# A four-layer network on one core: the spreading product and the state sums get due times of their own, single steps are queued by known work, and two tiles are doubled

## The chip, the cores and the metric

The kernel runs on one core of a Trainium2 chip. A core has TensorE (PE, matrix products into the PSUM memory), VectorE (DVE), ScalarE (ACT), GpSimd (POOL) and SyncE (SP, which here only issues DMAs). Each engine works through its own queue in the order in which the program was written out, and waits at the head of the queue until what the next instruction needs is there. The metric is the device time of one execution in microseconds, the median of the runs shown; less is better.

## What is computed

The input is `x` of shape 4 x 96 x 64 x 64 (4 images, 96 channels, 4096 pixels). Four layers are added to it, one after the other:

```python
x = x + _L0_conv_ref(_gn(x), ...)      # layer norm, 1x1 projection, 3x3 depthwise convolution, selective scan
x = x + _L1_conv_ref(_gn(x), ...)      # deformable 3x3 convolution, 4 bilinear corners for 9 taps
t = t + _L2_attn_ref(_ln_t(t), ...)    # FFT over the 4096 tokens, a product by channel, inverse FFT
t = t + _L2_ffn_ref(_ln_t(t), ...)     # 96 -> 384 -> 96 with quantized numbers
t = t + _L3_attn_ref(_ln_t(t), ...)    # attention without softmax, 6 heads
t = t + _L3_ffn_ref(_ln_t(t), ...)     # as the other one
```

The core of layer 0 is a recurrence along 4096 pixels, for 4 images, 4 directions, 192 channels and 16 states:

```python
dA = jnp.exp(d_t[..., None] * A)
h = dA * h + (d_t * u_t)[..., None] * b_t[:, :, None, :]
y = jnp.einsum('bkdn,bkn->bkd', h, c_t)
```

## The kernel before, in words

**Units of the scan.** The recurrence is cut into 1536 units (4 images x 4 directions x 4 stretches of 1024 pixels x 24 groups of 8 channels; 8 channels x 16 states fill the 128 partitions). `Layer0.scan` (L887) writes them out one after the other. A unit has these parts, each a method with a line of its own in the profile:

- `fetch` (L953) loads `da`, the step widths, 512 KB, from ACT's DMA queue (L982); `decay` (L1000) turns it into `exp(A * d)` on ACT (L1003).
- `inflow` (L1005) is the spreading product: two matmuls (L1009) that spread `du` of 8 channels over 128 partitions into the PSUM tile `db`. There are two `db` tiles, so the product of unit n+2 has to wait until the scan of unit n has read its tile.
- `enter` (L1018) multiplies `db` by `b_t` on DVE (L1023), and `recur` (L1025) runs the recurrence itself on DVE (L1031) into `hh`. There are six `hh` tiles.
- `weigh` (L1035) multiplies `hh` by `c_t` on POOL (L1040), and keeps the last state (L1038).
- `total` (L1042) is the state sums: for two units at a time, four matmuls (L1059) that add up the 16 states into the PSUM tile `py`; the first total of a block of eight units also adds an earlier result (L1054). An `hh` tile is free after its total. `settle` (L1067) copies `py` out on ACT (L1070), and `store` writes it.

**Side work.** Everything else is called side work here: the convolution (L752) and the gates of layer 0 for later images (`steps`, L812 to L884), the end of layer 0 (`behind`, L1081), layer 1 (`Layer1`; its samples are gathered at L1372 and transposed at L1405), and layers 2 and 3 (`Fourier`, `Ffn`, `LinearAttention`). It comes in two streams (L1792 on): `ends` holds the beginning of layer 0 and then layers 2 and 3 image by image; `middle` holds `behind` and layer 1 image by image. Layers 2 and 3 of an image begin when `middle` has sampled it.

**The order.** The whole order of instructions is decided while the program is built, by a planner in Python. Its `Clock` (L206) adds a fixed cost in us for every step to the end of the engine (`ends`), and gives every unit at least `PACE` = 4.5. After a unit of the scan, `yield True` (L949) hands over to the two streams, and as many side steps are written out as `has_room` (L231) lets in: an engine that the step uses may be planned at most `AHEAD` = 3, 3, 5 and 7 us (PE, DVE, ACT, POOL) past now, and DVE gets at most `BESIDE` = 6 us of side work for each unit. Inside a `pipe` (L272), which interleaves several chains of steps, `has_room` asks with the work that the same step had the last time. A single step outside a pipe is asked for in `Stream.step` (L331) with 1 us on all four engines, whatever it uses. Banks of PSUM for side work are counted too: three during the scan.

In iteration n, `scan` wrote out first `inflow` of unit n+1 and `decay` of unit n+2, on odd n `total` of units n-5 and n-4, then the loads, `recur` of unit n, `weigh` of unit n-2 and, where due, `settle` and `store`; then the side work of this iteration. `enter` of unit n+1 is written out either in the middle of the side work, ahead of a step that uses DVE, when the planner's clock has reached `entered` (the end of that unit's spreading product by the clock), or after the side work. The spreading product of unit n+1 therefore stood behind all side matmuls that were written out in iteration n-1.

**After the last unit** the banks of the scan go to the stream `ends` (`own_banks`, L1837), and what is left of the side work is written out alone: the end of layer 0 and layer 1 of the last image in one stream, layers 2 and 3 of the last images in the other.

**The doubled tiles.** In `steps`, the logarithm's tiles `lw` and `w1` (L833 to L842) exist once, and a token `lw=1` lets one chain at a time from the matmul at L829 to L842. In `Fourier.half`, the last stage (`last`, L1573) copies a product (L1579) to the single tile `yt` (L1581), which the next product reads (L1584); a token `yt=1` keeps a second chain from beginning its product before.

Of the kernel before, what the change touches and what calls it, by code (L numbers as in the profile page):

```python
# [1 line left out]

# [1 line left out]

# [4 lines left out]
F32 = mybir.dt.float32  # L9
# [10 lines left out]
B, C, H, W = 4, 96, 64, 64  # L20
# [174 lines left out]
PE, DVE, ACT, POOL = range(4)  # L195
# [10 lines left out]
class Clock:  # L206
# [4 lines left out]
    def __init__(self):  # L211
# [8 lines left out]

        self.enter, self.entered = None, 0.0

    def now(self):
        return max(self.ends[DVE], self.due) if self.own is None else self.own

# [15 lines left out]
    def precede(self, work):  # L241


        if self.enter and work[DVE] and self.own is None and self.entered + MARGIN <= self.ends[DVE]:
            self.enter()

    def add(self, engine, us, ready):
        self.ends[engine] = max(self.ends[engine], ready) + us
# [72 lines left out]
    yield wait(max(0.0, end - clock.now()))  # L321


class Stream:


# [4 lines left out]
    def step(self):  # L331

        net = self.net
        net.stream = self
        if self.over or self.ready > net.clock.now():
            return False
        if not self.piped and not (net.has_bank() and net.clock.has_room((1.0,) * 4, self.ready)):
            return False
        step = next(self.work, False)
        if step is False:  # L340
            self.over = True
            return False
        self.piped = step is None or step is BLOCKED
        if isinstance(step, Step):
            self.ready = net.clock.queue(step, net.clock.now())
        return step is not BLOCKED

# [195 lines left out]
class Layer0:  # L543
# [54 lines left out]
    def first(self):  # L598


        net = self.net
        tc, nc = net.tc, net.nc
        b = 0
        with tc.tile_pool(name=f"l0u{b}", bufs=1) as up, tc.tile_pool(name=f"l0b{b}", bufs=1) as sm:
            us = []
            x = self.tokens(b, up, us)
            xp_a, xp_c = (net.load(q, sm) for q in ("xp_a", "xp_c"))
            dtw = net.load("dtw", sm)
            xdbl = {}
            with tc.tile_pool(name=f"l0a{b}", bufs=1) as big, tc.tile_pool(name=f"l0i{b}", bufs=1) as cp:  # L610
                pad = big.tile([C, PW, PW], F32, name=f"pad{b}", tag="pad")
                weights = self.conv_weights(b, cp)
                yield from self.normed_rows(b, x, pad)

                def rows_first():
                    yield self.conv(b, 0, pad, us, weights, cp)
                    for j in range(NCH):
                        if j + 1 < NCH:
                            yield self.conv(b, j + 1, pad, us, weights, cp)
                        yield self.projected(b, j, us, xp_a, xp_c, sm, xdbl, (0,), f"c{j}")  # L620
                        for ks in ((0,), (0, 2), (2,)):
                            yield self.steps(b, ks, j, us, dtw, sm, xdbl)

                tokens = {f"c{j}": 0 for j in range(NCH)}
                yield from pipe(
                    net, rows_first(), 6, every=2, lane=Layer0.conv.__code__,
                    ex=3, lw=1, rl=2, du=2, zt=1, **tokens,
                )

            def columns():  # L630
                for j in range(NCH):
                    yield self.projected(b, j, us, xp_a, xp_c, sm, xdbl, (1,))
                    for ks in ((1,), (1, 3), (3,)):
                        yield self.steps(b, ks, j, us, dtw, sm, xdbl)

            yield from pipe(net, columns(), 5, every=2, ex=3, lw=1, rl=2, du=2)

    def before(self, b):
        net = self.net
        tc, nc, ins = net.tc, net.nc, net.ins  # L640
        with tc.tile_pool(name=f"l0u{b}", bufs=1) as up:

            us = []
            yield from self.inputs(b, up, us)
            with tc.tile_pool(name=f"l0b{b}", bufs=1) as sm:
                xp_a, xp_c = (net.load(q, sm) for q in ("xp_a", "xp_c"))
                dtw = net.load("dtw", sm)
                yield wait(4.0)
                xdbl = {}

                def chains():
                    yield self.projected(b, 0, us, xp_a, xp_c, sm, xdbl, (1, 0))
                    for j in range(NCH):
                        for ks in ((1,), (0, 1), (3,), (2, 3), (0,), (2,)):
                            yield self.steps(b, ks, j, us, dtw, sm, xdbl)
                        if j + 1 < NCH:
                            yield self.projected(b, j + 1, us, xp_a, xp_c, sm, xdbl, (1, 0))

                yield from pipe(self.net, chains(), 5, every=2, ex=3, lw=1, rl=2, du=2)

    @staticmethod
    def rows(pad, j):
# [149 lines left out]
    def steps(self, b, ks, j, us, dtw, sm, xdbl):  # L812

        net = self.net
# [5 lines left out]
        def tile_of(name, bufs):  # L820
            return sm.tile([128, CH], F32, name=f"{name}{tk}", tag=name, bufs=bufs)
# [5 lines left out]
        for i, k in enumerate(ks):  # L827
            o, m = (pd[64 * i : 64 * i + 64], slice(128, DI)) if both else (pd, slice(0, 128))
            nc.tensor.matmul(o, lhsT=dtw[:, k, m], rhs=xdbl[k % 2, j], start=True, stop=True)  # L829
        ex = tile_of("ex", 3)  # L830
        nc.scalar.activation(ex, pd, AF.Abs)
        nc.scalar.activation(ex, ex, AF.Exp, scale=-1.0)
        lw, w1 = tile_of("lw", 1), tile_of("w1", 1)  # L833
        nc.scalar.activation(lw, ex, AF.Ln, bias=net.one)
        nc.scalar.activation(w1, ex, AF.Identity, bias=net.one)
        yield cost(pe=2.2 if both else 1.1, act=2.7, holds=1, takes="rl")
        rl = tile_of("rl", 2)
# [49 lines left out]
    def scan(self):  # L887


        units = [  # L890
            Unit(b, k, step, g, i, q)
            for b in range(B)
            for k in ((1, 3, 0, 2) if b else (0, 1, 3, 2))
            for step in range(NT)
            for g in range(NG)
            for i in range(4)
            for q in range(2)
        ]
        ahead = 5
        loaded = 0  # L900
        clock = self.net.clock

        def at(m):
            return units[m] if 0 <= m < len(units) else None

        def made(u):
            return all(
                (u.b, u.k, both, 2 * u.j + h) in self.ready for both in (False, True) for h in range(2)
            )

        for n in range(len(units) + 7):
            for m in range(loaded, min(n + ahead + 1, len(units))):
                while not made(units[m]):
                    yield False
            if n == 0:
                while loaded < ahead:
                    self.fetch(units[loaded], units[loaded - 1] if loaded else None)
                    loaded += 1
                self.decay(at(0))
                self.decay(at(1))  # L920
                self.inflow(at(0))
                self.next = at(0)
                self.enter()

            for period, tick, load in ((24, 12, self.fetch_step), (8, 2, self.fetch_block)):
                u = at(n - n % period + period)
                if n % period == tick and u is not None and made(u):
                    load(u)
            for stage, m in ((self.inflow, n + 1), (self.decay, n + 2)):
                if at(m) is not None:  # L930
                    stage(at(m))
            if n % 2 == 1 and at(n - 5) is not None:
                self.total(at(n - 5), at(n - 4))
            if loaded < len(units):
                self.fetch(units[loaded], units[loaded - 1])
                loaded += 1
            if at(n) is not None:
                self.recur(at(n), at(n - 6).summed if n >= 6 else 0.0)
            if at(n - 2) is not None:
                self.weigh(at(n - 2))  # L940
            if n % 2 == 0 and at(n - 6) is not None and at(n - 6).i == 3:
                self.settle(at(n - 6))
            if n % 2 == 1 and at(n - 7) is not None and at(n - 7).i == 3:
                self.store(at(n - 7))
            clock.unit(self.scanned[1])
            self.next = at(n + 1)
            if self.next is not None:
                clock.enter, clock.entered = self.enter, self.next.spread
            yield True  # L949
            if clock.enter:  # L950
                self.enter()
# [483 lines left out]
class Fourier:  # L1435
# [6 lines left out]
    def __init__(self, ctx, net):  # L1442
# [14 lines left out]

        self.w2 = wp.tile([C + 1, 2, 128], F32, name="w2e")
        nc.sync.dma_start(self.w2[:C], ins["w2"])
        self.yt = wp.tile([C + 1, 8, 64], F32, name="yt")  # L1460

    def prepare(self, tp):
        net = self.net
# [63 lines left out]
    def half(self, key, g, tv, t, pool, big):  # L1527
# [45 lines left out]
        def last(m):  # L1573
# [3 lines left out]
            pt = net.mm(f"yp{key}_{m}", C).rearrange("p (q k) -> p q k", k=64)  # L1577
            for q in range(8):
                nc.tensor.matmul(pt[:, q, :], lhsT=d[:, m + q, :], rhs=m2[:, q, :], start=True, stop=True)  # L1579
            yt = self.yt  # L1580
            nc.scalar.copy(yt[:C], pt)  # L1581
            yield cost(pe=1.7, act=0.6, new=True)
            po = net.mm(f"o{key}_{m}").rearrange("p (q k) -> p q k", k=64)
# [2 lines left out]
            nc.vector.tensor_add(to[:, m : m + 8, :], to[:, m : m + 8, :], po[:C])  # L1586
            yield cost(dve=1.25)

        yield from pipe(self.net, (last(m) for m in range(0, 64, 8)), 4, yt=1)


def normed(net, t, tl, key, pool):
# [272 lines left out]
```

## Time and profile before

| | before |
|---|---|
| median of 3 runs | 8710.01 us (8709.18 to 8720.84) |
| the profiled execution's own time | 8725.68 us |
| its span, first to last instruction | 8723.9 us |
| mean granted TensorE clock | 0.779 |
| busy: PE, DVE, ACT, POOL | 6608.9, 6836.1, 4925.0, 5608.7 us |
| first spreading product, last scan | 187.3 us, 7507.4 us |
| DVE multiplication by `b_t` (L1023), recurrence (L1031) | 1214 ns and 2285 to 2344 ns each |

The profile is read in this way. A line of a group names the line of the code, the engine, the operation and the tiles (written `out<-in`), the number of instructions, their busy time and the mean of one in ns; behind the bar stands the time that the engine sat idle just before them, and what ended it. A line of waits says which engine and tile waited for which other one: us in total, number of times, the longest. A line of the timeline has the start in us, the duration in us, the instruction, and in brackets the idle time before it. In the table by stage each engine has its busy time and, in brackets, its number of instructions; then come the granted TensorE clock (1 is full speed), the busy share of the 16 DMA engines, and GB/s.

### The profile page before, as it was taken

Reading aid. Unit: us, or ns where it says so; the run is one execution under the profiler, and the core shown is the slowest. Engines: PE = TensorE matmul, PEld = TensorE weight load, DVE = VectorE, ACT = ScalarE, POOL = GpSimd, SP = SyncE. Lnnn points to the kernel's source line nnn. Section 1 sums busy time; section 2 is a strip of 40 time slices with the busy share of each in tenths; the row PEclk is TensorE's granted clock in tenths of the full one; section 3 lists DMA queues with packets and bytes.
Section 4 is the critical chain, followed back from the end, with each engine's and each line's share of the span. In section 5 each row is a group of like instructions: output and inputs, shape, how many; then the busy total and the mean of one; then the engine's idle time right before and its main releaser. Section 6 shows DMA issues by size and latency. Waiting matters only on the chain.

```text
span 8723.9 us, 97214 instructions
## 1 busy us (share of the span) xinstructions
PE 6608.9 (76%) x31960; PEld 2859.5 (33%) x31960; DVE 6836.1 (78%) x5155; ACT 4925.0 (56%) x9030; POOL 5608.7 (64%) x4291
## 2 busy tenths in 40 slices
PE   6675777759767777887676788777778887789697
PEld 2211221112222332321222245422335541267383
DVE  2799889978799898778799888788988888547514
ACT  5554566636467776555577666454766665322323
POOL 0465566656579898656588887565888877347200
PEclk9765787769667777886687788776778887788788
DMA  3677678877789999766799988866879997355110
GB/s 94 160 206 186 167 199 218 211 169 193 181 217 242 242 239 231 177 169 178 194 244 239 236 222 215 188 173 165 215 207 233 229 224 170 90 153 172 56 54 13
DMA packets 773820, 1608.33 MB, mean 184 GB/s; under 512 B 264065, under 2 KB 355741, under 8 KB 771206
## 3 DMA queue, kind: packets, MB, share of 16 engines
q10 hardware_dynamic: 244224, 843.17, 38.3%
q1 hardware_dynamic: 455366, 532.37, 23.7%
q0 software_dynamic: 73728, 226.57, 9.8%
q8 instruction: 257, 4.21, 0.2%
q14 instruction: 245, 2.01, 0.1%
HBM read 1345.43 MB, written 256.29 MB: 184 GB/s over the span
## 4 chain that ended last, share of the span: by engine, by line
PE 25%; DVE 15%; DMA 7%; ACT 5%; issue 4%; SPq 1%; POOL 1%; ACTq 1%; DVEq 0%; POOLq 0%
DVE hh L1031 7%; DVE db L1023 4%; PE f L1499 3%; PE ps L1405 3%; PE py L1059 3%; PE pd L1421 2%; DMA da<-de 2%; ACT g L1384 1%; PE db L1009 1%; PE pc L752 1%; PE h L1540 1%; PE yp L1579 1%; DMA m<-in_dft 1%; ACT da L1003 1%; PE lnc L474 1%
## 5 line engine op out<-in xcount | busy, mean ns | idle before, releaser
L1040 POOL TENSOR_TENSOR hh<-hh,bc 128x1024 f32<-128x1024 f32 x1536 | 3661.0, 2386 | 377.2 <-DVE hh L1031 274.3
L1031 DVE TENSOR_TENSOR_SCAN hh<-da,st,db 128x1024 f32<-128x1024 f32 x1152 | 2700.6, 2344 | 189.4 <-PE py L1059 74.0
L1023 DVE TENSOR_TENSOR db<-db,bc 128x1024 f32<-128x1024 f32 x1536 | 1864.0, 1214 | 604.4 <-PE db L1009 602.7
L1003 ACT ACTIVATE da<-da,w_al 128x1024 f32<-128x1024 f32 x1536 | 1737.5, 1145 | 511.8 <-DMA da<-de 168.1
L1372 POOL DMA_INDIRECT g<-table,idx x1152 | 1212.7, 1053 | 373.8 <-issue 173.6
L1009 PE MATMUL db<-du,rep 24*128 24x512 bf16 x3072 | 710.0, 461 | 858.3 <-DVE hh L1031 803.5
L1059 PE MATMUL py<-hh,w_fold 128*32 128x512 f32 x6144 | 1107.7, 796 | 16.2 <-issue 11.5
L1384 ACT ACTIVATE g<-g,wt 128x96 f32<-128x96 f32 x3456 | 963.6, 364 | 136.9 <-PE py L1059 34.3
L1031 DVE TENSOR_TENSOR_SCAN hh<-da,db 128x1024 f32<-128x1024 f32 x384 | 877.3, 2285 | 84.6 <-PE py L1059 40.7
L1405 PE MATMUL ps<-w_ident,g 128*96 128x128 f32 x3744 | 736.1, 342 | 176.3 <-ACT g L1384 101.2
L1009 PEld LDWEIGHTS <-rep 24*128 24x128 bf16 x3072 | 159.6, 94 | 1963.0 <-issue 1289.7
L1038 POOL COPY st<-hh 128x1 f32<-128x1 f32 x1152 | 235.0, 204 | 741.5 <-DVE hh L1031 688.6
L1405 PEld LDWEIGHTS ps<-w_ident,g 128*96 128x96 f32 x3744 | 511.3, 149 | 548.6 <-ACT g L1384 239.0
L840 POOL TENSOR_TENSOR lw<-lw,w 128x512 f32<-128x512 f32 x192 | 243.9, 1270 | 683.7 <-DVE w L838 649.0
L752 PE MATMUL pc<-pad,wc 96*128 96x512 f32 x1152 | 579.6, 643 | 32.7 <-DMA wc<-wc_d 23.3
L871 PE MATMUL pr<-ex,w_ident 128*128 128x512 f32 x384 | 305.7, 889 | 174.7 <-DVE ex L861 81.9
L1413 ACT COPY st<-ps 96x384 f32<-96x384 f32 x384 | 178.8, 472 | 422.0 <-PE ps L1405 385.5
L752 PEld LDWEIGHTS pc<-pad,wc 96*128 96x128 f32 x1152 | 221.0, 202 | 361.5 <-issue 314.3
L829 PE MATMUL pd<-xd,w_dtw 103*64 103x512 f32 (+1 forms) x512 | 275.7, 821 | 52.7 <-DVE rl L842 18.8
L1421 PE MATMUL pd<-st,wdc 96*128 96x256 f32 x1152 | 308.9, 419 | 1.3 <-DVE d L1548 1.1
L1508 ACT COPY d<-f 128x512 f32<-128x512 f32 x192 | 111.9, 583 | 301.8 <-PE f L1499 297.1
L1059 PEld LDWEIGHTS py<-hh,w_fold 128*32 128x32 f32 x6144 | 158.5, 125 | 355.2 <-issue 282.9
(252 smaller groups left out, 8915.4 us busy)
## 6 DMA issues: line engine op xcount, KB each, us to landing
da<-de ACTq DMA_DIRECT2D x1536, 512.0 KB
du<-du SPq DMA_DIRECT2D x1536, 96.0 KB
bc<-bcd SPq DMA_DIRECT2D x128, 512.0 KB
y<-yb SPq DMA_DIRECT2D x384, 128.0 KB
de<-rl SPq DMA_DIRECT2D x128, 256.0 KB
m<-in_dft SPq DMA_DIRECT2D x128, 256.0 KB
ad<-y ACTq DMA_DIRECT2D x192, 128.0 KB
table<-pix SPq DMA_DIRECT2D x256, 96.0 KB
```

What stands on the lines that cost most here:

```text
L752: nc.tensor.matmul(pp, lhsT=wc[:, q, g * 128 : (g + 1) * 128], rhs=pad[:, r0 + dy : r0 + dy + NR, dx : dx + W], start=(q == 0), stop=(q == 8),
L871: nc.tensor.matmul(pr, lhsT=net.ident, rhs=ex, start=True, stop=False)
L1003: self.net.nc.scalar.activation(u.da, u.da, AF.Exp, scale=self.al[:, a : a + 1])
L1009: self.net.nc.tensor.matmul(db[:, h, :], lhsT=self.rep[64 * u.q + 32 * h : 64 * u.q + 32 * h + 24], rhs=u.du[64 * u.q + 32 * h : 64 * u.q ...
L1023: self.net.nc.vector.tensor_mul(u.db, u.db, u.bc[:, 0, :])
L1031: nc.vector.tensor_tensor_scan(u.along(u.hh), u.along(u.da), u.along(u.db), first, ALU.mult, ALU.add)
L1040: self.net.nc.gpsimd.tensor_mul(u.hh, u.hh, u.bc[:, 1, :])
L1059: nc.tensor.matmul(py[p0 : p0 + 32], lhsT=self.fold[:, u.i, :], rhs=hc[:, h * CH : (h + 1) * CH], start=u.sums["add"] is None and u.i == 0 ...
L1372: nc.gpsimd.indirect_dma_start(out=g[:, k, :], out_offset=None, in_=self.tables[b % 2], in_offset=bass.IndirectOffsetOnAxis(ap=idx[:, n : ...
L1384: nc.scalar.activation(pixel, pixel, AF.Identity, scale=wt[:, n, c : c + 1])
L1405: nc.tensor.matmul(pt[:, k, :], lhsT=g[:, k, c * C : (c + 1) * C], rhs=net.ident, is_transpose=True, start=(c == 0), stop=(c == corners - 1),)
L1421: nc.tensor.matmul(po, lhsT=wdc[:, k, :], rhs=st[:, k, :], start=(k == 0), stop=(k == 8))
```

## The change

It has four parts.

1. **Due times.** The clock gets a list `early`. At the end of iteration n, `scan` appends the spreading product of unit n+2, due when the planner's clock of PE reaches the end of the scan of unit n (`scanned[1]`), and on even n the total of units n-4 and n-3, due when both are weighed (and, for the first of a block, `py` is settled). `precede`, which is called ahead of each side step of a pipe, writes out what is due before a step that uses PE. What has not come up by the beginning of iteration n+1 is written out there, in the old place.
2. **Single steps.** `Stream.step` looks up, by the place in the code at which the stream stands (`place`), which work the step from there had the last time, and asks `has_room` with that. The first time it asks with 1 us on all engines as before. A step that is only a wait then needs no room.
3. **`lw` and `w1` get two buffers each**, and the token is 2.
4. **`yt` gets two halves**, taken in turn, and the token is 2.

No instruction is added or removed, and every side step does what it did.

```diff
+        self.early = []
...
         if self.enter and work[DVE] and self.own is None and self.entered + MARGIN <= self.ends[DVE]:
             self.enter()
+        if work[PE] and self.own is None:
+            for due in [e for e in self.early if e[0] <= self.ends[PE]]:
+                self.early.remove(due)
+                due[1]()
...
+def place(steps):
+
+    while steps.gi_yieldfrom is not None and hasattr(steps.gi_yieldfrom, "gi_code"):
+        steps = steps.gi_yieldfrom
+    return steps.gi_code, steps.gi_frame.f_lineno
...
-        if not self.piped and not (net.has_bank() and net.clock.has_room((1.0,) * 4, self.ready)):
+        here = place(self.work) if self.work.gi_frame else None
+        work = net.known.get(here, (1.0,) * 4)
+        if not self.piped and not (net.has_bank() and net.clock.has_room(work, self.ready)):
             return False
...
         if isinstance(step, Step):
+            if not self.piped:
+                net.known[here] = step.work
             self.ready = net.clock.queue(step, net.clock.now())
...
-                    ex=3, lw=1, rl=2, du=2, zt=1, **tokens,
+                    ex=3, lw=2, rl=2, du=2, zt=1, **tokens,
...
-        lw, w1 = tile_of("lw", 1), tile_of("w1", 1)
+        lw, w1 = tile_of("lw", 2), tile_of("w1", 2)
...
-            for stage, m in ((self.inflow, n + 1), (self.decay, n + 2)):
-                if at(m) is not None:
-                    stage(at(m))
-            if n % 2 == 1 and at(n - 5) is not None:
-                self.total(at(n - 5), at(n - 4))
+            while clock.early:
+                clock.early.pop(0)[1]()
+            if n == 0:
+                self.inflow(at(1))
+            if at(n + 2) is not None:
+                self.decay(at(n + 2))
...
+            if at(n + 2) is not None:
+                clock.early.append((self.scanned[1], partial(self.inflow, at(n + 2))))
+            if n % 2 == 0 and at(n - 4) is not None:
+                u, v = at(n - 4), at(n - 3)
+                clock.early.append((max(u.weighed, v.weighed, self.settled if u.i == 0 else 0.0), partial(self.total, u, v)))
             yield True
...
-        self.yt = wp.tile([C + 1, 8, 64], F32, name="yt")
+        self.yt = wp.tile([C + 1, 2, 8, 64], F32, name="yt")
...
-            yt = self.yt
+            yt = self.yt[:, m // 8 % 2]
...
-        yield from pipe(self.net, (last(m) for m in range(0, 64, 8)), 4, yt=1)
+        yield from pipe(self.net, (last(m) for m in range(0, 64, 8)), 4, yt=2)
```

More of the change, by code (lines that the diff above doesn't have):

```diff
@@ L1 @@
 from contextlib import ExitStack
+from functools import partial
 import numpy as np
@@ L634, in columns @@
                         yield self.steps(b, ks, j, us, dtw, sm, xdbl)
-            yield from pipe(net, columns(), 5, every=2, ex=3, lw=1, rl=2, du=2)
+            yield from pipe(net, columns(), 5, every=2, ex=3, lw=2, rl=2, du=2)
     def before(self, b):
@@ L657, in chains @@
                             yield self.projected(b, j + 1, us, xp_a, xp_c, sm, xdbl, (1, 0))
-                yield from pipe(self.net, chains(), 5, every=2, ex=3, lw=1, rl=2, du=2)
+                yield from pipe(self.net, chains(), 5, every=2, ex=3, lw=2, rl=2, du=2)
     @staticmethod
```

## The prediction, as it was put on record

> **What bounds the kernel now.** First I read the table by stage, cut at the first spreading product, the last scan and the end of sampling.
>
> ```profile
> 187.00:7507.00 7320.00, 5513.34 (x24611) 2146.92 (x24612) 6241.70 (x4238) 4456.49 (x8155) 5230.06 (x3963) 0.76 0.80 203
> 7507.00:8180.00 673.00, 547.95 (x3912) 379.89 (x3904) 393.19 (x564) 208.04 (x421) 361.96 (x312) 0.85 0.46 130
> 8180.00:8724.00 544.00, 423.24 (x3173) 283.44 (x3172) 168.66 (x293) 166.20 (x331) 7.66 (x2) 0.86 0.11 33
> ```
>
> The columns are PE, weight loads, DVE, ACT and POOL. The scan takes 7320 us, and in it DVE is busy for 6241.7, more than any other engine, and idle for 1078. So time can be won there only by closing DVE's gaps. After it DVE is busy for 58% and then 31%: there the chain goes through other engines. The waits say who opens the gaps (us, times, longest):
>
> ```profile
> PE db L1009 <- DVE hh L1031: 803.5, 429, 20.5
> ...
> DVE db L1023 <- PE db L1009: 602.7, 262, 26.0
> ...
> DVE hh L1031 <- PE py L1059: 114.8, 95, 8.1
> ```
>
> 602.7 of the 1078 us are DVE waiting for a spreading product, 114.8 for state sums (a free `hh` tile). The first line is the reverse: PE at the head of its queue waiting until a scan has freed a `db` tile. The timelines of PE and of DVE show one gap:
>
> ```profile
> 3721.13 0.60 PE L1009 MATMUL db<-du,rep 24*128 24x512 bf16 x2
> 3721.66 7.06 PE L752 MATMUL pc<-pad,wc 96*128 96x512 f32 x8
> 3728.66 0.39 PE L1009 MATMUL db<-du,rep 24*128 24x512 bf16 x2
> 3728.97 1.07 PE L1059 MATMUL py<-hh,w_fold 128*32 128x512 f32 x8
> ```
>
> ```profile
> 3723.15 2.35 DVE L1031 TENSOR_TENSOR_SCAN hh<-da,st,db 128x1024 f32<-128x1024 f32 x1
> 3729.09 1.23 DVE L1023 TENSOR_TENSOR db<-db,bc 128x1024 f32<-128x1024 f32 x1 [3.60 <-PE db L1009]
> ```
>
> Two `db` matmuls of 0.39 us stand behind 7.06 us of convolution; their tile had been free since before 3721.8, yet DVE, done at 3725.5, waits 3.60 us.
>
> Last, the final image's inverse Fourier stage:
>
> ```profile
> 8518.59 0.58 ACT L1581 COPY yt<-yp 96x512 f32<-96x512 f32 x1 [2.60 <-PE yp L1579]
> ...
> 8519.23 1.13 PE L1584 MATMUL o<-yt,w2e 97*128 97x512 f32 x2 [0.72 <-ACT yt L1581]
> ...
> 8520.19 1.50 PE L1579 MATMUL yp<-i,d 128*96 128x64 f32 x16
> ```
>
> PE idles 0.72 us in each round for the copy.
>
> **The change part by part.** The sum is made against the profiled execution's 8725.68 us (span 8723.9 plus 1.8), which is 15.7 above the median 8710.01.
>
> *Spreading products earlier.* From the built instruction order of both kernels I took, for each unit m, the side matmuls written out between scan m-2, which frees the tile, and the product of m, each at its line's mean PE time in the trace. Before: mean 3.24 us, 6.61 at the 90th percentile. After: 2.40 and 4.65. The product gains 0.84 us of lead, about 2 where the queue is longest. I set that against DVE's waits for it, counted singly in the trace from 0.15 us: 105 under 1 us (51 us in all), 56 of 1 to 2 (80), 81 of 2 to 5 (249), 19 longer (197). A lead of 0.84 takes about 45 from the first class and 56 x 0.84 = 47 from the second; about 1.4 each takes 113 from the third; 2 each takes 38 from the last, which is mostly PE standing still behind a side step whose load or POOL work is late. That is 243. Not all reaches the end: a scan that starts earlier meets its `da`, its `hh` or the next product sooner. Between all of it and a quarter (60) I take six tenths, since DVE's gaps have no second cause of this size: -146.
>
> What is queued behind it: the product waits for its scan at the head of PE's queue, and side matmuls stand behind. PE is free for 7320 - 5513 = 1807 us of the scan, of which 803 are such waits already; I count the rest as cover. Without it, see the rival below.
>
> [...] The rows show mean waits of 1.87 us (803.5/429), and 1004 us of PE's time that no `db` wait fills[...].
>
> *State sums earlier.* In the built order 44 of the 765 totals now come two units ahead of the old place, and 70 fewer come in the last possible one. Between 0 and -115 I take -35, a third, since most stay.
>
> *Two tiles for the gates, known work for single steps.* ACT waits for `lw` 66.5 us (49 times), DVE for `w` 38.8 in the scan. But ACT is busy for only 61% of it, and more chains compete for the same order. From +40 to -66 I take -5, near the DVE row. Single steps issue loads and norms sooner; the built order has image 1's Fourier transform begin at unit 1241 instead of 1315. That pays only at the end.
>
> *What is moved from the end into the scan.* Before, image 1's attention and second feed-forward are still open at the last scan; after, they are done, and so are 10 of 16 hidden groups of image 2's first half. In the scan they cost DVE 16 x 0.67 (L1603) + 8 x 1.54 (L1684) + 8 x 0.73 (L1740) + 10 x 0.54 (L1548) + 6 for two inverse roots = 41, and PE about 100, which PE's free time hides. DVE is the bound: +41. Their POOL and ACT steps lie in those engines' slack, and their loads (image 2's tokens, 1.5 MB, moved past SP's queue) come where DMA is 0.65 to 0.8 busy; both 0, up to +10.
>
> *The end.* Before, image 2's Fourier stage starts 192 us after the last scan (7699), and image 2 ends at 747 (8254), 100 us after the last sampled pixel at 647 (8154); only then is image 3 loaded. After, its Fourier stage runs from the start, so it ends at about 747 - 192 = 555 and sampling becomes the last: image 3 starts at 647, -100. Fourier matmuls now run beside the offset convolutions of image 3 (L1267), which may delay sampling by 0 to 40; I take 15: -85. With two `yt` halves the built order has pairs of products, so the 0.72 us are covered in 16 rounds of the last image: -11, I take -10.
>
> Sum: -146 - 35 - 5 + 41 - 85 - 10 = -240. 8725.7 - 240 = 8486 for a profiled execution; the median goes from 8710 to **8470**.
>
> **The rivals.**
>
> *The wait moves.* DVE gets its product sooner and waits as long for something else: side steps that stand behind PE's new waits, or `da`, whose DMAs share engines 0.80 busy, over 0.90 in the sampling stretches. Speaks for it: in the table by stage, from 2500 to 3250, DVE is already busy for 92% and POOL for 89%. Against it: in the trace six tenths of the waits for products lie outside the sampling stretches (2500 to 3500, 4250 to 5500, 6000 to 7250). Then only the end gains: -95 + 41 = -54, 8656.
>
> *The lead is enough.* Once PE is ahead it stays ahead. All waits under 5 us for products go (380) and half of those for sums (57): -437 + 41 - 110 = -506, 8204. For it: PE has 1807 us free. Against it: side bursts like the 7.06 us above remain.
>
> *Slower: PE's queue is blocked.* In the sum over 1534 units the products move ahead of 4974 - 3675 = 1300 us of side matmuls. If PE reaches each of them early and stands there, its waits grow by 1300: 5513 + 803 + 1300 = 7616 against 7320, +296 on the scan. With the end's -95 that is 8911. It decides from 1004 us of new waits on, 77% of the 1300; below that PE's free time takes it. Against it: a product is written out only once the clock puts PE past the scan.
>
> *It does nothing:* the due times are mostly not reached and the order stays. The built order excludes most of that: 61% of the products now stand ahead of the scan before them, against 43%. 8710.
>
> **How the numbers follow.** Chances: the forecast 0.62, the wait moves 0.17, the lead is enough 0.12, nothing 0.03, blocked 0.06. The forecast's own bounds: -243 to -60 for products, -115 to 0 for sums, -66 to +40 for tiles, [...]-125 to -50 for the end; taken together, since they don't all fall on one side, 8350 to 8590. To leave out no more than 2 in 10, the range runs from 8290, part of the way to the second rival, to 8660, which takes in the first. A measurement of this kernel tells about 0.2% (17 us) from no change: faster 0.91, same 0.03, slower 0.06.
>
> **What would show it.** Right: DVE's wait for `db` at about 350 to 450 us instead of 603; PE's wait for the scan at 900 to 1500, up from 803; the last scan at about 7360; image 3's load about 650 us after it instead of 750; rounds of the `yt` stage without PE's 0.72. Wrong: `db` waits gone but the scan as long (the wait moved), side work's waits on DVE far above the scan's 214 us, a granted clock well below 0.76, or sampling ending later than 690 us after the last scan.

## The result, and the profile after

The changed kernel takes 8602.1 us (median of 4 runs, 8574.27 to 8630.86). The ratio to the kernel before is 0.9871, 95% interval 0.9837 to 0.9905: 113 us faster than the kernel before, whose median with a fourth run is 8715.0, where 240 were forecast. The profiled execution took 8605.6 us (span 8603.8), 120.1 less than the one before. Line numbers have moved: the spreading product is L1033, its multiplication L1047, the scan L1055, the sums L1083 (L1078 at the start of a block).

The table by stage of the changed kernel, cut at its first and last scan and at the load of image 3 (PE, weight loads, DVE, ACT, POOL, clock, DMA share, GB/s):

```profile
180.00:7516.00 7336.00, 5572.59 (x25022) 2188.87 (x25023) 6290.54 (x4290) 4505.53 (x8269) 5252.58 (x3980) 0.77 0.80 203
7516.00:8170.00 654.00, 529.93 (x3650) 373.61 (x3647) 376.68 (x540) 197.75 (x401) 364.48 (x311) 0.82 0.47 131
8170.00:8604.00 434.00, 359.52 (x3028) 253.35 (x3028) 126.35 (x217) 137.29 (x270) 3.83 (x1) 0.90 0.13 37
```

The scan is not shorter: 7336 us against 7319. The last scan ends at 7516.2, before at 7509.7. The gain lies behind it: 1087.6 us against 1214.1, which is 126.5 less. Ahead of it another 10 us are gone (the first scan starts at 180.3 instead of 190.3), and the scan itself gives 16.5 back. DVE's waits inside the scan:

```profile
DVE hh L1055 <- PE py L1083: 323.0, 132, 14.8
DVE db L1047 <- PE db L1033: 247.9, 95, 22.9
DVE hh L1055 <- ACT da L1027: 82.7, 62, 11.0
```

Waits for products have fallen from 602.7 to 247.9. Waits for sums have risen from 114.8 to 323.0 and those for `da` from 13.3 to 82.7. PE's wait for the scan is 763.5, before 803.5. One gap in the timelines of PE and of DVE, in the same kind of stretch as the one shown before:

```profile
3689.62 0.39 PE L1033 MATMUL db<-du,rep 24*128 24x512 bf16 x2
3690.46 4.56 PE L770 MATMUL pc<-pad,wc 96*128 96x512 f32 x10 [0.46 <-ACT xa L780]
3694.95 1.07 PE L1078 MATMUL py<-ad,w_ident 128*32 128x512 f32 x8
3695.84 1.04 PE L1083 MATMUL py<-hh,w_fold 128*32 128x512 f32 x8
```

```profile
3690.05 1.23 DVE L1047 TENSOR_TENSOR db<-db,bc 128x1024 f32<-128x1024 f32 x1 [0.39 <-PE db L1033]
3697.08 2.35 DVE L1055 TENSOR_TENSOR_SCAN hh<-da,st,db 128x1024 f32<-128x1024 f32 x1 [5.80 <-PE py L1083]
```

The product now stands ahead of the convolution and DVE multiplies almost at once. But the sums that free an `hh` tile still stand behind it, and the scan waits 5.80 us for them. Where DVE used to wait ahead of the multiplication, it waits behind it.

At the end, PE's idle time in the inverse Fourier stage of the last image is gone, as forecast:

```profile
8400.50 2.93 PE L1603 MATMUL yp<-i,d 128*96 128x64 f32 x32 [0.67 <-ACT d L1532]
8403.27 1.96 PE L1608 MATMUL o<-yt,w2e 97*128 97x512 f32 x4
8405.06 2.86 PE L1603 MATMUL yp<-i,d 128*96 128x64 f32 x32
```

Two rounds take 4.56 us (8400.50 to 8405.06), 2.28 each against 3.18 before, and PE no longer idles between them. The image has two such stages, one for each half, and each takes 18.4 us now, at a granted clock of 1.00. Before, they took 41.1 and 25.7 us, and the clock (third number from the end) was not the same in both:

```profile
8385.00:8426.00 41.00, 35.25 (x146) 24.89 (x146) 8.76 (x7) 4.65 (x8) 0.00 (x0) 0.53 0.18 52
8514.00:8540.00 26.00, 19.71 (x144) 14.25 (x143) 9.38 (x8) 4.65 (x8) 0.00 (x0) 1.00 0.13 42
```

In that one execution the first stage, at 0.53, took 15 us longer than the second, at 1.00, for the same instructions. The changed kernel ran both at 1.00.

### The profile page after: what moved, and what is told of

The parts are those of the page before. It is cut to its first block, busy times and chain, and to the rows that moved or that the text cites. A ratio compares the mean times of both kernels' runs of the same rounds, so it can differ in the third digit from the quotient of the medians.

```text
span 8603.8 us, 97099 instructions
## 1 busy us (share of the span) xinstructions
PE 6578.8 (76%) x31960; PEld 2861.9 (33%) x31960; DVE 6827.1 (79%) x5107; ACT 4934.5 (57%) x9062; POOL 5629.9 (65%) x4307
## 4 chain that ended last, share of the span: by engine, by line
PE 26%; DVE 18%; DMA 7%; ACT 7%; issue 4%; POOL 1%; SPq 1%; ACTq 1%; DVEq 0%; POOLq 0%
DVE hh L1055 9%; DVE db L1047 4%; PE f L1523 4%; PE ps L1429 3%; PE py L1083 3%; PE pd L1445 2%; ACT g L1408 2%; ACT da L1027 2%; DMA da<-de 1%; PE db L1033 1%; DMA m<-in_dft 1%; PE pc L770 1%; PE h L1564 1%; PE zp L1589 1%; PE py L1078 1%
## 5 line engine op out<-in xcount | busy, mean ns | idle before, releaser
L1055 DVE TENSOR_TENSOR_SCAN hh<-da,st,db 128x1024 f32<-128x1024 f32 x1152 | 2700.0, 2344 | 390.8 <-PE py L1083 231.2
L1047 DVE TENSOR_TENSOR db<-db,bc 128x1024 f32<-128x1024 f32 x1536 | 1857.1, 1209 | 249.0 <-PE db L1033 247.9
L1033 PE MATMUL db<-du,rep 24*128 24x512 bf16 x3072 | 714.4, 459 | 806.2 <-DVE hh L1055 763.5
L1083 PE MATMUL py<-hh,w_fold 128*32 128x512 f32 x6144 | 1100.9, 780 | 22.5 <-ACT yb L1094 7.4
L1055 DVE TENSOR_TENSOR_SCAN hh<-da,db 128x1024 f32<-128x1024 f32 x384 | 877.0, 2284 | 166.7 <-PE py L1083 91.7
L1033 PEld LDWEIGHTS <-rep 24*128 24x128 bf16 x3072 | 169.3, 94 | 2075.1 <-issue 966.6
L1429 PE MATMUL ps<-w_ident,g 128*96 128x128 f32 x3744 | 689.1, 335 | 192.3 <-ACT g L1408 54.5
L1445 PE MATMUL pd<-st,wdc 96*128 96x256 f32 x1152 | 331.7, 438 | 6.6 <-DVE rl L860 5.5
L1083 PEld LDWEIGHTS py<-hh,w_fold 128*32 128x32 f32 x6144 | 162.4, 125 | 431.2 <-issue 315.0
```

Of the source, the lines that this page charges most:

```text
L1033: self.net.nc.tensor.matmul(db[:, h, :], lhsT=self.rep[64 * u.q + 32 * h : 64 * u.q + 32 * h + 24], rhs=u.du[64 * u.q + 32 * h : 64 * u.q ...
L1047: self.net.nc.vector.tensor_mul(u.db, u.db, u.bc[:, 0, :])
L1055: nc.vector.tensor_tensor_scan(u.along(u.hh), u.along(u.da), u.along(u.db), first, ALU.mult, ALU.add)
L1083: nc.tensor.matmul(py[p0 : p0 + 32], lhsT=self.fold[:, u.i, :], rhs=hc[:, h * CH : (h + 1) * CH], start=u.sums["add"] is None and u.i == 0 ...
L1429: nc.tensor.matmul(pt[:, k, :], lhsT=g[:, k, c * C : (c + 1) * C], rhs=net.ident, is_transpose=True, start=(c == 0), stop=(c == corners - 1),)
L1445: nc.tensor.matmul(po, lhsT=wdc[:, k, :], rhs=st[:, k, :], start=(k == 0), stop=(k == 8))
```

## The experiments

The runs were made on chips of different speed (the kernel before took 8690 to 8798 us on them), so ratios to the kernel before on the same chip are compared; times inside a profile only within one group, and where another group's stand beside them this is said.

**First group (kernel before 8795.1).** e1 undoes part 1:

```diff
-            while clock.early:
-                clock.early.pop(0)[1]()
...
+            for stage, m in ((self.inflow, n + 1), (self.decay, n + 2)):
+                if at(m) is not None:
+                    stage(at(m))
+            if n % 2 == 1 and at(n - 5) is not None:
+                self.total(at(n - 5), at(n - 4))
```

> The changed kernel with part 1 undone: products and sums stand in their old places, single steps and doubled tiles as changed. In the built order even more side work lies ahead of the last scan than in the changed kernel (5241 instructions behind it, against 5753). Theory A (the due times only exchange one wait of DVE for another, and the gain is all in the end, from parts 2 to 4): the last scan ends within 30 us of the kernel before's 7510, DVE waits about 600 us for products and 110 for sums, the part after the scan is about 1085 us, and the time is that of the changed kernel, 8602, within 30. Theory B (the due times shorten the scan, and the side work that was moved in lengthens it by as much): the last scan ends 100 us or more later than the changed kernel's 7516, time 8700 or more.

Measured: ratio 0.9854 (0.9827 to 0.9880), no different from the changed kernel's 0.9871. The last scan ends at 7555, outside the 30 us of theory A, and the median is 8664.1, but this chip is the slower one (the kernel before takes 8795.1 us on it, 8715.0 on the other). The end takes 1106 us. The waits are those of the kernel before:

```profile
DVE db L1041 <- PE db L1027: 593.1, 263, 29.7
DVE hh L1049 <- PE py L1077: 97.1, 98, 4.8
```

So beside parts 2 to 4 the due times bring nothing that can be measured: the two kernels of this group that have them, e4 and e2 below, take 8683.9 and 8710.9 us. What part 1 would do alone was not run.

e4 keeps due times for products alone; the sums go back to the beginning of the odd unit:

```diff
-            if n % 2 == 0 and at(n - 4) is not None:
-                u, v = at(n - 4), at(n - 3)
-                clock.early.append(...)
...
+            if n % 2 == 1 and at(n - 5) is not None:
+                self.total(at(n - 5), at(n - 4))
```

> The changed kernel, but only the spreading products have due times; the sums are written out at the beginning of the odd unit, as before. 5712 instructions stand behind the last scan (5753 in the changed kernel). Theory A: the exchange of waits is as in the changed kernel or stronger: products about 250, sums 320 to 450, last scan 7500 to 7560, time 8590 to 8650. Theory C expects the same sign: sums alone late. If the sums' own due times mattered, the time is 50 us or more above the changed kernel's.

Measured: ratio 0.9871 (0.9845 to 0.9898).

```profile
DVE hh L1054 <- PE py L1082: 511.9, 203, 21.0
DVE db L1046 <- PE db L1032: 142.2, 53, 24.9
```

The exchange in its purest form, and stronger than expected: against e1, products -451, sums +415, and no gain in time.

e2 and e3 go together. e2 only changes the planner's sum; e3 also queues each sum one unit earlier:

```diff
-        ... self.net.clock.add(PE, 1.5 + 1.3 * (u.i == 0), ready)
+        ... self.net.clock.add(PE, 1.5 + 1.3 * (u.i == 0), 0.0)
 e3 alone:
-            if n % 2 == 0 and at(n - 4) is not None:
-                u, v = at(n - 4), at(n - 3)
+            if n % 2 == 1 and at(n - 3) is not None:
+                u, v = at(n - 3), at(n - 2)
...
-            if n % 2 == 0 and at(n - 6) is not None and at(n - 6).i == 3:
-                self.settle(at(n - 6))
+            if n % 2 == 1 and at(n - 5) is not None and at(n - 5).i == 3:
+                self.settle(at(n - 5))
```

> The changed kernel, but the planner's clock no longer lets PE's end wait for the weighing of the units summed (only the planner's sum is changed; each sum still waits for its data). A control for the next run: side work ahead of the last scan is about that of the next one (5329 and 5320 instructions behind it). Theory A: waits for products 200 to 350, for sums 300 to 450, last scan within 40 us of 7516, time 8580 to 8640. Theory C (the sums are the last obstacle): the same here, as the sums' latest place is unchanged.

> As the control, and each state sum is queued one unit earlier (due at the end of the odd unit before, settle with it), so that it stands ahead of one more unit's side matmuls. Theory C (DVE's wait went from the products to the sums, since these stand behind the same side matmuls, and nothing else holds DVE): wait for sums below 130 us, for products still about 250, last scan near 7350, time 8420 to 8480. Theory D (PE's queue itself is what DVE waits for: any product or sum drawn ahead makes another one or a side result late): wait for sums falls, but waits for products, da or side results grow by as much, last scan 7480 to 7540, time 8570 to 8640.

Measured: e2 0.9897 (0.9872 to 0.9923), e3 0.9713 (0.9686 to 0.9740); scans of 7419 and 7260 us. e2 is slower than expected (its last scan ends at 7605). In e3 the waits for sums are gone, products are at 351.7 and `da` at 140.6; its last scan, at 7445, and its time, 8548.7, lie between the two theories. Drawing the second of the two forward gives part of the gain that the first alone did not.

**Second group (kernel before 8699.5).** e5 asks for single steps with `(1.0,) * 4` again, e6 sets `lw`, `w1` and the token back to 1:

```diff
 e5:
-        work = net.known.get(here, (1.0,) * 4)
+        work = (1.0,) * 4
 e6:
-        lw, w1 = tile_of("lw", 2), tile_of("w1", 2)
+        lw, w1 = tile_of("lw", 1), tile_of("w1", 1)
```

> The changed kernel with part 2 undone: single steps are asked for with 1 us on all engines again. 6225 instructions stand behind the last scan, as in the kernel before (6203), so image 1's attention and second feed-forward are back in the end. If the gain is all in the end and comes from what was moved out of it: the part after the scan is about 1190 to 1210 us (the doubled yt tile saves some 15), waits for products 250, for sums 320 as changed, ratio to the kernel before 0.994 to 1.002. If the due times gain by themselves: ratio below 0.992.

> The changed kernel with part 3 undone: lw and w1 exist once. 6143 instructions stand behind the last scan, nearly as before (6203): the move out of the end needs part 3 as well as part 2. Same expectations as for the run without part 2: ratio 0.992 to 1.000 if only the end counts, below 0.992 if the due times gain by themselves.

Measured: e5 0.9973 (0.9962 to 0.9985), e6 0.9919 (0.9896 to 0.9942); the end takes 1207 and 1170 us. Without part 2 most of the gain is gone and the end is nearly as long as before (1214). Without part 3 the end lies between (1088 with all parts), and 0.8 of the 1.3% remain: the whole move out of the end needs both parts. e6 lies on the border of its two expectations. Its scan, 7248 us, is 72 shorter than in the profile before, and that of e5, 7293, is 26 shorter; both have the due times, and about as much side work behind the scan as the kernel before. So with the old amount of side work part 1 may gain something. How much is open: these are single executions, set beside one on another chip.

e7 leaves the products in their old place and queues the sums one unit earlier, as in e3.

> State sums one unit earlier as in the run e3, but the spreading products in the place of the kernel before; parts 2 to 4 kept, 5220 instructions behind the last scan. If DVE is held by whichever of the two stands behind the side matmuls (theory C): waits for products back at about 550 to 600, for sums below 60, last scan as in e1 (the run without due times), ratio 0.983 to 0.989. If the early sums alone make the gain of e3: ratio 0.975 or less.

Measured: 0.9848 (0.9820 to 0.9876), as e1. There are no waits for sums, and products are back:

```profile
DVE db L1045 <- PE db L1031: 610.4, 297, 25.0
```

Neither half alone shows a gain over e1: e4 on the same chip, e7 on another.

e8 is e3 with products due 1.5 us sooner (`self.scanned[1] - 1.5`).

> As e3 (sums one unit earlier), and the products due 1.5 us earlier on the planner's clock. 5562 instructions behind the last scan. Theory C: waits for products fall from 352 to 150 to 250, sums stay below 60, ratio 0.955 to 0.968. Theory D (PE's queue gives back what it gains): PE's wait for the scan rises from 690 above 850, side results come late, ratio 0.968 to 0.980.

Measured: 0.9817 (0.9794 to 0.9840), outside both expectations. Products stayed at 340.3, and PE's wait for the scan is 749.4. What PE does while DVE waits for a product has changed: by the trace of e8 it is side work for 144 us, sums for 82, the products themselves for 72, and idle for 44. In the scan of the kernel before it was 346, 8, 101 and 123. The sums now stand ahead of the products.

**Third group (kernel before 8689.6).**

> The changed kernel itself, on the same chip as the next three, so that their ratios to the kernel before can be set side by side. Every theory: ratio 0.984 to 0.990, scan as long as the kernel before's within 40 us, waits for sums and products together 500 to 620 us.

> The kernel of e3 (due times for products, sums one unit earlier) beside the changed kernel on one chip. Theory C: a ratio 0.008 to 0.020 below that of the changed kernel, from a scan that is 60 to 160 us shorter. If e3's gain was its chip's: within 0.004 of it.

Measured: e9, the changed kernel, 0.9893 (0.9871 to 0.9914); e10 0.9807 (0.9784 to 0.9831), scans of 7322 and 7259 us. e10 takes 8529 us against 8596, and is faster than both kernels. The granted clock in its scan is 0.79 against 0.77 in e9; what of the gain is owed to that was not separated. e10 is also the kernel of e3, whose ratio on the other chip was 0.9713: here a ratio carried over from chip to chip only to about 0.01. That both halves together gain is safe, since each chip shows it by itself (against e1, and against e9).

e11 queues `decay` one unit earlier than e10, that of unit n+3 in place of n+2.

> As e10, and decay is queued one unit earlier on ACT (unit n+3 in place of n+2), since in e3 DVE waits 141 us for it. If that wait is real and nothing takes its place: wait of the scan for ACT's da below 60, ratio 0.005 to 0.015 below e10's. If PE's queue gives it back (theory D): da's wait gone, waits for products or side results up by as much, ratio within 0.004 of e10's.

Measured: 0.9927 (0.9904 to 0.9950). DVE's waits in e10, then in e11:

```profile
DVE db L1047 <- PE db L1033: 364.2, 185, 16.0
DVE hh L1055 <- ACT da L1027: 151.2, 114, 6.4
```

```profile
DVE db L1048 <- PE db L1034: 579.6, 244, 27.1
```

The wait for `da` has fallen to 11.9, and products have risen by 215: again one wait for another, here with a loss. Why the products came so much later was not traced.

e12 sets `yt` back to one half and the token to 1.

> The changed kernel with part 4 undone: yt exists once; the order up to the last scan is nearly that of the changed kernel. The last image's two inverse Fourier stages take 0.7 us more in each of 16 rounds, so the part from its load to the end is 8 to 30 us longer than the changed kernel's 434; ratio 0.001 to 0.004 above the changed kernel's.

Measured: 0.9941 (0.9919 to 0.9963), 0.0048 above e9, where up to 0.004 were expected. From image 3's load to the end 451 us against e9's 434: 17, as expected; the two inverse Fourier stages take 25.7 us each instead of 18.4; the mean clock from the last scan to the end is 0.86, in e9 0.87. The scan is longer by 55 us, and these have all come by unit 1016, up to which the orders are the same; `yt` is first used after it. So it was not part 4, and what it was is open. Two executions of one order on one chip lay that far apart in the scan here.

**Fourth group (kernel before 8798.0).** e13 computes two of the nine taps of layer 0's convolution; all costs and the order stay:

```diff
+                if q % 8 == 0:
                     nc.tensor.matmul(pp, ...)
```

> The changed kernel with 7 of the 9 taps of layer 0's convolution left out (only the first and the last are computed, so the activations are other numbers); the order of everything else is the same. It takes about 450 us of side matmuls (7/9 of 579.6) out of PE's queue, some 400 of them in the scan. Theory D (DVE waits for PE's queue as a whole): the scan gets 120 to 300 us shorter than the changed kernel's, ratio 0.95 to 0.975, and DVE's waits for products and sums together fall from about 570 to below 420. If PE's 1760 idle us in the scan are real slack: the scan within 50 us of the changed kernel's, ratio 0.983 to 0.990.

Measured: 0.9733 (0.9712 to 0.9755). The scan in e13, and in e9 for comparison:

```profile
159.00:7411.00 7252.00, 5329.56 (x24197) 2059.58 (x24229) 6275.00 (x4289) 4505.21 (x8269) 5256.38 (x3980) 0.75 0.80 206
```

```profile
185.00:7508.00 7323.00, 5553.04 (x25022) 2193.67 (x25023) 6288.79 (x4292) 4504.89 (x8269) 5252.94 (x3981) 0.77 0.80 204
```

DVE's waits in e13 (e9 has 254.2 for products and 306.5 for sums):

```profile
DVE hh L1056 <- PE py L1084: 272.3, 117, 16.2
DVE db L1048 <- PE db L1034: 191.1, 68, 21.7
```

The ratio is inside what theory D expects; the waits have fallen less than it expects. The scan is 71 us shorter than e9's, but e9 ran on the faster chip: e13's end, from which nothing was left out, is 71 us longer than e9's (1138 against 1067). By the ratios (0.9733 against the changed kernel's 0.9871 and 0.9893) e13 would be 120 to 140 us faster than the changed kernel on its own chip. 26 of these lie ahead of the first scan (at 159 instead of 185), which leaves some 100 for the scan. This is a rough estimate, since the changed kernel was not run on this chip. PE's idle time is thus not plain slack, and PE's queue is one of the things that hold DVE; that it is the only one is not shown.

e14 and e15 have parts 3 and 4 undone, and in their place e15 has a seventh `hh` tile (`bufs=6` to `bufs=7`). On every engine the instructions stand in the same order in both.

> The changed kernel with parts 3 and 4 undone, a control for the next run, whose seventh hh tile needs their memory. 6123 instructions behind the last scan. Waits for sums about 300, products 200 to 280, ratio 0.992 to 1.000.

> The same order as the control, instruction by instruction, but with seven hh tiles instead of six: a state sum may be one unit later before the scan waits for it. Theory C (the exchange from products to sums took the gain, and the sums are the last obstacle): wait for sums from about 300 to below 120, scan 100 to 200 us shorter, ratio 0.012 to 0.024 below the control. Theory D: the wait for sums falls as far, but products, da and side results rise, so that DVE's idle time falls by less than 70 us; ratio within 0.008 of the control.

Measured: e14 0.9948 (0.9928 to 0.9967), e15 0.9866 (0.9837 to 0.9895). DVE's waits in e14, then in e15:

```profile
DVE hh L1055 <- PE py L1083: 300.5, 134, 10.8
DVE db L1047 <- PE db L1033: 231.7, 99, 17.6
DVE hh L1055 <- ACT da L1027: 61.1, 54, 9.2
```

```profile
DVE db L1047 <- PE db L1033: 423.2, 190, 25.3
DVE hh L1055 <- ACT da L1027: 116.8, 110, 9.2
```

With no instruction moved, 300.5 us of waits for sums are gone; 191.5 come back as waits for products and 55.7 for `da`. The scan is 38 us shorter and DVE's idle time 60. This is theory D by the idle time; the ratio, 0.008 below the control, lies on its edge and short of theory C. The two profiled executions are 17 us apart and the medians 77 (8672.1 against 8749.4), so 38 us may be too little for what the seventh tile brings; the exchange takes back most, not all.

**Side by side**, DVE in the scan (us). "Side results" are waits of side work on DVE. "Other" are waits of the multiplication and the scan that the profile puts down to none of these three. The rows come from different chips, named by the time of the kernel before:

| | chip | scan | DVE busy | idle | products | sums | da | side results | other |
|---|---|---|---|---|---|---|---|---|---|
| before | 8715 | 7319 | 6243 | 1076 | 603 | 115 | 13 | 214 | 14 |
| changed | 8715 | 7336 | 6291 | 1045 | 248 | 323 | 83 | 250 | 41 |
| e1 no due times | 8795 | 7371 | 6271 | 1100 | 593 | 97 | 34 | 211 | 42 |
| e4 products only | 8795 | 7364 | 6234 | 1130 | 142 | 512 | 46 | 212 | 127 |
| e7 sums only | 8699 | 7304 | 6279 | 1025 | 610 | 0 | 28 | 247 | 5 |
| e10 both | 8690 | 7259 | 6251 | 1008 | 364 | 0 | 151 | 353 | 7 |
| e11 both, decay early | 8690 | 7378 | 6286 | 1092 | 580 | 0 | 12 | 352 | 4 |
| e14 six `hh` | 8798 | 7272 | 6223 | 1049 | 232 | 300 | 61 | 284 | 53 |
| e15 seven `hh` | 8798 | 7234 | 6245 | 989 | 423 | 0 | 117 | 304 | 45 |

Single waits change by hundreds of us; the sum of all of them goes from 876 (e10) to 1039 (e4). Each row is one execution, and e9 and e12 put two of one order 55 us apart. So the exchange between columns is clear of that spread, while differences of 30 to 60 us in the scan are not.

## Why the prediction was wrong, point by point

The time lies within the range that was given, 8290 to 8660, but not for the reason given. The scan was to get 145 us shorter and got 17 longer; the end was to get 95 shorter and got 126.5 shorter, 15 of them beside a low clock in the one profiled execution before: 0.53 in a stage of 41.1 us, whose twin took 25.7 us at 1.00.

- **What bounds the scan.** Right that DVE is the fullest engine (6290.5 of 7336 us, PE 5572.6) and that its gaps are the reserve; wrong that closing the largest gap closes time.
- **Products earlier: the step that failed.** "Not all reaches the end ... I take six tenths, since DVE's gaps have no second cause of this size: -146." The lead itself worked better than assumed: -355 instead of -243. But there was a second cause of this size: the state sums, which PE also comes to late. 114.8 us was not its size but what was left visible behind the first. In the 323 us that DVE now waits for sums, PE is busy with the sums themselves for 184, with side work for 83, with products for 15, and idle for 41. Of the 355 us, products, sums and `da` together kept 77 (731 to 654), and DVE's idle time 31, where products, sums and tiles were to take 186 from it. That waits for products turn into waits for sums and `da` is shown by e4 against e1 and, with no instruction moved, by e15 against e14.
- **State sums: -35.** Measured +208. I read their lead off the order (70 of 765 moved) but did not ask what the wait becomes once DVE arrives sooner.
- **Side work moved into the scan: +41.** DVE's busy time rose by 47 (6243.2 to 6290.5).
- **Tiles and single steps: -5 in the scan.** Not to be told apart. Their worth is at the end, where e5 and e6 show that the whole gain needs both.
- **The granted clock.** One well below 0.76 was to speak against the forecast. In the scan it is 0.77, where it was 0.76, and PE's waits for the scan are shorter: 494 of 1.55 us on average (763.5 us), before 429 of 1.87 (803.5). That longer waits of PE would lower the clock is not shown by any run here; the room left for it in the range was my own estimate.
- **The end: -95.** Measured -126.5. Image 3 is loaded 654 us after the last scan instead of 752 (-98, taken as -85: the last sample is transposed 646 us after the last scan, before 639, so sampling was delayed by 7 and not by 15). From there to the end it is 434 instead of 462, -28 instead of -10. The second `yt` half gives 15 of these: each of the two stages takes 18.4 us instead of 25.7, as e12, e14 and e15 with one half have it, and a round is 0.90 us shorter where I counted only PE's idle 0.72. Another 15 are the length of the first stage before, at a clock of 0.53, over the second, at 1.00; in the changed kernel both ran at 1.00.
- **The rivals.** In the scan, "the wait moves" came true (+17 us against its +41), though I looked for the wait at `da` and side results and it came mostly to the sums. Its 8656 was above the result because the end gained more. "The lead is enough" sets -110 for the end, where the sum has -95; nothing hangs on the 15. PE's queue was not blocked: its waits for the scan fell from 803.5 to 763.5 us.
- **How finely it can be told.** The 0.2% was too fine: the interval came out at 0.34% to each side, and the runs of e12 alone reach from 8598 to 8695.

What stays open is what sets the sum of some 900 us. e13 shows PE's queue to be part of it. What holds the remainder was not tried.

## What to carry to other kernels

When an engine waits for two things that stand in the same queue of another engine, the profile shows the second only by what the first leaves of it: here 115 us, and 512 once the first was drawn forward. Drawing one forward gained nothing; drawing both gained about 1%, and going on from there (e8, e11) gained nothing clear or lost. To size such a gain, add up all waits of the bound engine, not the one that is addressed: an extra buffer at unchanged order is a cheap way to see what comes next. And work that is moved out of a stretch with another bound can be worth all of the gain (here the end became 126.5 us shorter) while the part that was meant to bring it gives none (the scan became 16.5 us longer).

## What the runs showed of the hardware that was not expected

In e13, 784 of the 1008 convolution matmuls in the scan are left out, some 395 us at the mean of the profile before (579.6 us for 1152). PE's busy time is only 223 us below that of e9 and 233 below that of e4, which ran on a chip as slow as that of e13 (the kernel before takes 8795.1 and 8798.0 us on them). The granted clock in the scan is 0.75, where every other run has 0.76 to 0.79. On e13's own chip, in e14 (clock 0.77), a matmul of the sums takes 779 ns on average and one of a product 460; in e13 they take 810 and 470. So leaving out some 395 us of matmuls, by that estimate, took only 223 to 233 us from PE's busy time, and the rest ran at a lower clock. What lowered it was not shown.

The low clock at the end of the kernel before, 0.53 through a stage of 41 us, came in rounds in which PE idled for no more than 0.73 us at a time. The second stage of the same execution had the same idle times and was granted 1.00. What set the clock apart was not found.
